# Router logits in the shared expert's unused columns, and three changes of order, in an attention and mixture-of-experts kernel on Trainium2

## The chip, the cores and the metric

The kernel runs on one core of one Trainium2 chip, as one launch. The metric is device time in microseconds. Before the change, three runs took 1483.86, 1485.7 and 1485.82 us, so the median is 1485.7 us. All times inside the kernel come from one profiled execution.

## The reference: what is computed

The input is x of 8 sequences, 512 tokens each, 256 numbers per token, all in fp32. Two residual blocks follow each other:

```python
x = x + _layernorm(attn(_layernorm(x), wq, bq, wkv, bkv, wo))
x = x + _layernorm(ffn(_layernorm(x), gate_w, w_gate, w_up, w_down, sh_gate, sh_up, sh_down))
...
# attn: 16 query heads of 128 in 4 groups, one key and value head per group, causal
q, k = q + pe, k + pe
probs = softmax(where(causal, q @ k.T / sqrt(128), -inf))
out = (probs @ v) @ wo
...
# ffn: all 4096 tokens together
scores = softmax(x @ gate_w.T)                 # 64 experts
topk_w, topk_idx = top_k(scores, 6)            # an expert takes its first 64 tokens, the rest are dropped
d = (silu(buf @ w_gate) * (buf @ w_up)) @ w_down
y = sum of the chosen experts' d, weighted
y = y + (silu(x @ sh_gate.T) * (x @ sh_up.T)) @ sh_down.T   # shared expert, 352 wide
```

## The kernel before, in words

The order of every engine's instructions is written out by hand (`manual_schedule`): the order of the Python calls is the order on PE, DVE, ACT, POOL and SP, and each engine works through its own list in order. The main loop (line 884) runs over 128 heads, k = 16 b + s with sequence b (0 to 7) and head s (0 to 15). One turn of it issues:

- `scores(k, 0..3)`, L273: the products psc (L280), DVE's e and its row minimum (L284), ACT's exponential (L287). Between the second and the third, `turned(k-1)`, L303: DVE transposes 32x32 blocks of the weights of the head before (L313), SP stores them to ex_d (L317) and loads them back as et (L320).
- `weigh(k)`, L291: reciprocal on DVE (L294), the scaling on POOL (L297).
- place A of the side work, `project(k-3)` (po, L352), place B, and a step of the routed experts where they are active (from k = 94 on).
- `queries(k+1)`, L263: the products pq (L267) and DVE's qt (L270), for which the next head's psc waits.
- `mix(k-2)`, L334: the products pav (L340) and ACT's copy ao.
- place D of the side work, and one unit of the preparation of the next sequence.

**Side work of a sequence.** `feed_forward(b-1)` makes a table of steps, keyed by head and place ("7A" is place A of head 7): residual and norm (2D to 5B), `turn` (6A: transposes pt_f into xt2, L118), `gate` (7A), `route` steps "r" (8D, 9D, 10A on) and `shared` steps "f" (8A, 8B, 9A, 9B, 11A, 11B, 12A, 13A on). `route` (L368) begins with the router's logits: 8 products pg = xt2 (stationary, 128 columns) times gw_sb (moving, 64 columns), L373, then a maximum on DVE (L376) and four exponentials on ACT (L380). `shared` (L661) computes the shared expert in chunks of 128, 128 and 96 columns (`SH_CHUNKS`): products psg and psu (L671) with the weights sg_sb and su_sb as stationary side and xt2 as moving side (512 columns), tanh on ACT (L676), two DVE products into hid (L678, L679); then the products py with sd_sb (L684). An fp32 product shows as two matmul records ("passes"), a transpose as one.

**Preparation of a sequence.** `prepare(b)` (L216) yields 12 units: load of x (`rows`), statistics (`scales`, st_a), `normal` (xn, L105), `turn` (pt_a into xnt), four `keys` (pk, L239, and kt, L242) and four `values` (pv, L250, and v, L252). For sequence 0 all 12 run ahead of the loop (L873), then `queries(0)`. For the others they run one per place: 5D, 6D, 7B (L904), 7D, 8D to 15D.

**Experts.** `experts()` (L612) works on pairs of experts from k = 94 to sequence 7's first heads; weights come by DMAs issued on ACT's queue. When all are done, `finish_early` (L864) finishes sequences 0 to 4 one after the other: SP loads two halves of y from y_d and x1 from x1_d (L650, L658), DVE adds y (L653), statistics (L76), then in `output` shift and scale on ACT (L96), POOL's additions (L641) and a store (L643).

**Tail.** `last_part` (L788) handles sequence 7 after the loop, with what is left of sequence 6 between its lines: `shared6()` is the next step of sequence 6's `shared` (8 steps, none of them done before the tail), `output6()` the next of its output, and `spare` what is left of `finish_early`. PSUM has three banks "s" (`ps_s`) and three "m" (`ps_m`); the string given to `shared` ("mmssms") says which one each of psg and psu takes.

**Loads.** SP issues x of sequence 0, then wkv, bk, bq, pe, bv, wq (one load of 2 MB), wo, gate_wt, the shared expert's weights (L146 to L159). x of a later sequence takes the buffer of the one two before it, so its load waits for that one's store to x1_d.

## Time and profile before

| | before |
|---|---|
| runs, median | 1485.7 us |
| the profiled execution's own time | 1494.1 us |
| its span, first to last instruction | 1492.3 us |
| mean granted PE clock | 0.982 |
| pg, sequences 0 to 6 (L373, 112 passes) | 13.3 us busy, 272 ns each |
| pg, sequence 7 (16 passes) | 3.9 us busy, 428 ns each |
| psg and psu (L671), mean of one pass of 512 columns | 592 ns |
| first psc, of head k = 0 | 28.29 us |
| first psc of k = 4, 16, 96, 112, 127 | 55.15, 163.33, 968.20, 1225.97, 1400.24 us |
| last po of the attention (L352) | 1418.14 us |
| last DMA issue, L643 | 1480.29 us |

Busy times are sums of the single durations, and matmuls overlap in their pipeline: 16 passes of pg start within 1.73 us though each lasts 272 ns. So the cost of products is read from start to start. In a timeline, the columns are start, duration, engine, line, operation, output and inputs, shape, count, and in brackets the idle time before and what ended it. "PEclk" is the granted share of PE's full clock; the first record of it in this execution is at 13.1 us.

### The profile page before, as it was taken

How to read it: one execution, taken by the hardware profiler on the slowest of the kernel's cores; microseconds unless marked ns; L12 is line 12 of the kernel's file. 1: busy time of each engine (PE TensorE's matmuls, PEld its weight loads, DVE VectorE, ACT ScalarE, POOL GpSimd, SP SyncE). 2: the span in 40 equal slices, each digit the busy share in tenths (PEclk: the TensorE clock that was granted, in tenths of full speed). 3: DMA queues.
4: the chain of work that ended last, by engine and by line, in shares of the span. 5: the costliest groups of instructions: out<-in, count | busy, mean ns of one | idle time of the engine just before them, and what ended most of it. 6: DMA issues, size and time to landing. Idle time of an engine off the chain costs nothing. (4 is left out here: it accounts for less than half of the span.)

```text
span 1492.3 us, 18593 instructions
## 1 busy us (share of the span) xinstructions
PE 1409.6 (94%) x5350; PEld 860.8 (58%) x5350; DVE 890.7 (60%) x3094; ACT 499.5 (33%) x1434; POOL 427.4 (29%) x682
## 2 busy tenths in 40 slices
PE   7999999999999999999999999988899998898894
PEld 3566655666656665666566666554555655565652
DVE  4565576657665676557665766665455454567442
ACT  1333343233332342233323332232333343344322
POOL 1222231124112322123112321144434344534202
PEclk9999999999999999999999999999999999999987
DMA  5764554355544464355435544469998899777511
GB/s 204 220 192 140 153 169 139 106 155 166 147 139 134 147 185 124 121 159 173 136 104 160 164 146 125 138 190 247 240 243 224 241 255 248 175 239 220 179 43 65
DMA packets 159702, 252.03 MB, mean 169 GB/s; under 512 B 16092, under 2 KB 135869, under 8 KB 159341
## 3 DMA queue, kind: packets, MB, share of 16 engines
q1 hardware_dynamic: 130061, 206.76, 46.5%
q10 hardware_dynamic: 23392, 34.61, 8.3%
q0 software_dynamic: 6144, 9.44, 3.4%
q8 instruction: 44, 0.72, 0.2%
q14 instruction: 61, 0.50, 0.1%
HBM read 143.01 MB, written 107.74 MB: 168 GB/s over the span
## 5 line engine op out<-in xcount | busy, mean ns | idle before, releaser
L297 POOL TENSOR_SCALAR e<-e,recip 128x128 f32<-128x128 f32 x508 | 269.6, 570 | 814.5 <-DVE recip L294 781.6
L287 ACT ACTIVATE e<-e,least 128x128 f32<-128x128 f32 (+3 forms) x512 | 285.8, 559 | 387.3 <-DVE least L284 356.0
L280 PE MATMUL psc<-kt,qt 128*128 128x128 f32 (+3 forms) x1024 | 312.7, 445 | 27.6 <-DVE least L284 8.7
L340 PE MATMUL pav<-et,v 128*128 128x512 f32 (+3 forms) x1024 | 297.2, 433 | 6.8 <-ACT dd L576 5.0
L340 PEld LDWEIGHTS pav<-et,v 128*128 128x128 f32 x1024 | 194.0, 190 | 170.1 <-issue 121.0
L284 DVE CUSTOM_DVE_ANT_0 e<-psc,mask 128x128 f32<-128x128 f32 (+3 forms) x512 | 231.7, 479 | 55.5 <-PE psc L280 49.6
L352 PE MATMUL po<-wo_sb,ao 128*128 128x256 f32 x1024 | 244.3, 382 | 0.7 <-ACT ao L108 0.7
L267 PE MATMUL pq<-xnt,wq_sb 128*128 128x512 f32 x512 | 240.8, 593 | 0.0
L352 PEld LDWEIGHTS po<-wo_sb,ao 128*128 128x128 f32 x1024 | 193.5, 191 | 69.3 <-issue 38.6
L280 PEld LDWEIGHTS psc<-kt,qt 128*128 128x128 f32 x1024 | 167.7, 193 | 108.7 <-DVE least L284 31.7
L313 DVE STREAM_TRANSPOSE eb<-e 128x128 f32<-128x128 f32 x756 | 227.4, 364 | 0.1
L108 ACT COPY ao<-pav 128x512 f32<-128x512 f32 x128 | 75.0, 586 | 445.3 <-PE pav L340 429.2
L270 DVE SCALAR_TENSOR_TENSOR qt<-pq,bq_sb,pe_sb 128x512 f32<-128x512 f32 x128 | 95.6, 747 | 115.0 <-PE pq L267 114.9
L267 PEld LDWEIGHTS pq<-xnt,wq_sb 128*128 128x128 f32 x512 | 95.9, 190 | 69.0 <-issue 63.5
L287 ACT ACTIVATION_READ_ACCUMULATOR e<-e,least 128x1 f32 x512 | 95.7, 187 | 0.0
L294 DVE RECIPROCAL recip<-total 128x4 f32<-128x4 f32 x128 | 22.8, 178 | 121.7 <-ACT e L287 121.7
L577 POOL DMA_INDIRECT y_d<-dd,idx x32 | 51.0, 1593 | 108.0 <-DMA y_d<-dd,idx 43.3
L239 PE MATMUL pk<-xnt,wkv_sb 128*128 128x512 f32 x128 | 61.3, 605 | 0.0
L252 DVE TENSOR_TENSOR v<-pv,bv_sb 128x512 f32<-128x512 f32 x32 | 22.1, 692 | 65.2 <-PE pv L250 65.2
L250 PE MATMUL pv<-wkv_sb,xnt 128*128 128x512 f32 x128 | 59.7, 593 | 0.0
L111 DVE COPY ht<-pth 88x256 f32<-88x256 f32 x32 | 13.4, 418 | 69.5 <-PE pth L558 69.4
L242 DVE SCALAR_TENSOR_TENSOR kt<-pk,bk_sb,pe_sb 128x512 f32<-128x512 f32 x32 | 24.0, 751 | 50.4 <-PE pk L239 50.4
(191 smaller groups left out, 1126.5 us busy)
## 6 DMA issues: line engine op xcount, KB each, us to landing
ex_d<-eb SPq DMA_DIRECT2D x126, 640.0 KB
et<-ex_d SPq DMA_DIRECT2D x504, 160.0 KB
wgu<-in_w_gate ACTq DMA_DIRECT2D x32, 352.0 KB
wgu<-in_w_up ACTq DMA_DIRECT2D x32, 352.0 KB
wd<-in_w_down ACTq DMA_DIRECT2D x32, 352.0 KB
y<-y_d SPq DMA_DIRECT2D x10, 512.0 KB
x<-in_x SPq DMA_DIRECT2D x8, 512.0 KB
x_d<-x SPq DMA_DIRECT2D x8, 512.0 KB
```

Of the source, the lines that this page charges most:

```text
L108: nc.scalar.copy(dst, src)
L239: nc.tensor.matmul(pk, lhsT=wkv_sb[:, c, g, 0, :], rhs=s["xnt"][:, c, :], start=c == 0, stop=c == NC - 1)
L250: nc.tensor.matmul(pv, lhsT=s["xnt"][:, c, ts(i, P)], rhs=wkv_sb[:, c, :, 1, :], start=c == 0, stop=c == NC - 1)
L267: nc.tensor.matmul(pq, lhsT=wq_sb[:, c, ts(h, D)], rhs=seqs[b]["xnt"][:, c, :], start=c == 0, stop=c == NC - 1)
L270: nc.vector.scalar_tensor_tensor(qt, pq, bq_sb[:, h : h + 1], pe_sb, ALU.add, ALU.add)
L280: nc.tensor.matmul(psc[:, :w], lhsT=l["qt"][:, ts(i, P)], rhs=seqs[b]["kt"][h // QPG][:, :w], start=True, stop=True)
L284: nc.vector.tensor_tensor_reduce(out=e, in0=psc[:, :w], in1=mask[:, T - w :], scale=-1.0 / math.sqrt(D), scalar=BIG, op0=ALU.add, op1=ALU. ...
L287: nc.scalar.activation(e, e, AF.Exp, bias=l["least"][:, i : i + 1], scale=-1.0, accum_out=l["total"][:, i : i + 1])
L297: engine.tensor_scalar(e, e, recip[:, n : n + 1], 1.0, ALU.mult, ALU.mult)
L313: nc.vector.transpose(blocks.rearrange("p c j t -> p j c t"), l["e"][i][:, js[0] * P : (js[-1] + 1) * P].rearrange("p (j c t) -> p j c t", ...
L340: nc.tensor.matmul(pav[:, :, j:, :], lhsT=seqs[b]["v"][:, j, ts(g, D)], rhs=l["et"][:, :, AT[j] : AT[j] + NI - j, :], start=j == 0, stop=j ...
L352: nc.tensor.matmul(po[b][i // 2][:, i % 2, :], lhsT=ao[:, ts(i, P)], rhs=wo_sb[:, h, :], start=h == 0 and i % 2 == 0, stop=h == NH - 1, sk ...
```

## The change

1. The router's weights are loaded into 32 free columns each of sg_sb and su_sb, behind the 352 of the shared expert. The chunk of 96 becomes 128 wide in psg and psu, and is now the first of the three. Its last 32 rows in each are the logits, transposed: ACT copies them into lg (64 x 512), and `route` turns them back with four transposes instead of eight products. The first chunk of `shared` moves to 7A and 7B, `gate` to 8A; this holds for sequence 6 too, whose `shared` ran in the tail entirely. In the tail, sequence 7's first chunk comes ahead of `route`.
2. Of sequence 0's preparation, only the first five units and the first values run ahead of the loop; the other six run in heads 0 to 3. wq is loaded in four parts by group.
3. 28 products of the identity with itself are put ahead of everything on PE.
4. For sequence 7 (prepared in sequence 6) the statistics move from 6D to 7D, normalization from 7B to 8B, and what follows by one place each, with one more unit at 14B. The load itself stays at 5D.
5. `spare` moves in the tail from before the last `output6()` to behind the first chunk of sequence 7.

```diff
@@ -36,6 +36,7 @@
 NEG = -3.0e38
 BIG = 3.0e38
 ROW = E + NX
+WARM = 28
 EARLY = 5
 ET_ROWS = EARLY * T
 LROW = ROW + NX
@@ -144,16 +145,24 @@
             return t
 
         x_first = load_x(0)
+
+        warm = ps_s.tile([P, T], F32, tag="s", name="warm")
+        for n in range(WARM):
+            nc.tensor.matmul(warm[:, :P], lhsT=ident, rhs=ident, start=True, stop=True)
         wkv_sb = load(wkv.rearrange("(c p) (g k d) -> p c g k d", p=P, g=G, k=2), [P, NC, G, 2, D], "wkv_sb")
         bk_sb = load(bk_t, [D, G], "bk_sb")
         bq_sb = load(bq_t, [D, NH], "bq_sb")
         pe_sb = load(pe_t, [D, T], "pe_sb")
         bv_sb = load(bv.partition_broadcast(P), [P, G * D], "bv_sb")
-        wq_sb = load(wq.rearrange("(c p) n -> p c n", p=P), [P, NC, NH * D], "wq_sb")
+        wq_sb = [load(wq[:, ts(g, QPG * D)].rearrange("(c p) n -> p c n", p=P), [P, NC, QPG * D], f"wq_sb{g}")
+                 for g in range(G)]
         wo_sb = load(wo.rearrange("(h d) e -> d h e", d=D), [D, NH, E], "wo_sb")
-        gw_sb = load(gate_wt.rearrange("(c p) n -> p c n", p=P), [P, NC, NX], "gw_sb")
-        sg_sb = load(sh_gate_t.rearrange("(c p) n -> p c n", p=P), [P, NC, FSH], "sg_sb")
-        su_sb = load(sh_up_t.rearrange("(c p) n -> p c n", p=P), [P, NC, FSH], "su_sb")
+
+        sg_sb, su_sb = [wpool.tile([P, NC, FSH + NX // 2], F32, tag=name, name=name) for name in ("sg_sb", "su_sb")]
+        for half, (t, w) in enumerate(((sg_sb, sh_gate_t), (su_sb, sh_up_t))):
+            nc.sync.dma_start(out=t[:, :, :FSH], in_=w.rearrange("(c p) n -> p c n", p=P))
+            nc.sync.dma_start(out=t[:, :, FSH:],
+                              in_=gate_wt.rearrange("(c p) n -> p c n", p=P)[:, :, ts(half, NX // 2)])
         sd_sb = wpool.tile([P, len(SH_CHUNKS), E], F32, tag="sd_sb", name="sd_sb")
         for n, (f0, fw) in enumerate(SH_CHUNKS):
             nc.sync.dma_start(out=sd_sb[:fw, n, :], in_=sh_down_t[ds(f0, fw), :])
@@ -264,7 +273,7 @@
             b, h = divmod(k, NH)
             pq = ps_m.tile([P, T], F32, tag="m", name=f"pq_{k}")
             for c in range(NC):
-                nc.tensor.matmul(pq, lhsT=wq_sb[:, c, ts(h, D)], rhs=seqs[b]["xnt"][:, c, :],
+                nc.tensor.matmul(pq, lhsT=wq_sb[h // QPG][:, c, ts(h % QPG, D)], rhs=seqs[b]["xnt"][:, c, :],
                                  start=c == 0, stop=c == NC - 1)
             qt = p2.tile([D, T], F32, tag="qt", name=f"qt_{k}")
             nc.vector.scalar_tensor_tensor(qt, pq, bq_sb[:, h : h + 1], pe_sb, ALU.add, ALU.add)
@@ -365,13 +374,12 @@
                                             imm_value=0.0)
                 yield
 
-        def route(b, xg, xt2):
-
+        def route(b, xg, l):
+
+            lg = l.pop("lg")
             pg = ps_m.tile([P, NI, NX], F32, tag="m", name=f"pg_{b}")
             for i in range(NI):
-                for c in range(NC):
-                    nc.tensor.matmul(pg[:, i, :], lhsT=xt2[:, c, ts(i, P)], rhs=gw_sb[:, c, :],
-                                     start=c == 0, stop=c == NC - 1)
+                nc.tensor.transpose(pg[:, i, :], lg[:, ts(i, P)], ident[:NX, :NX])
             most = small.tile([P, NI], F32, tag="most", name=f"most_{b}")
             nc.vector.tensor_reduce(most, pg, AX.X, ALU.max, negate=True)
             sc = p1.tile([P, NI, NX], F32, tag="sc", name=f"sc_{b}")
@@ -662,15 +670,21 @@
 
             hid = p1.tile([P, len(SH_CHUNKS), T], F32, tag="hid", name=f"hid_{b}")
             banks = iter(banks)
-            for n, (f0, fw) in enumerate(SH_CHUNKS):
+
+            for n, (f0, fw) in reversed(list(enumerate(SH_CHUNKS))):
+                mw = min(P, fw + NX // 2)
                 pgu = []
                 for w_sb, name in ((sg_sb, "psg"), (su_sb, "psu")):
                     tag = next(banks)
                     pp = {"m": ps_m, "s": ps_s}[tag].tile([P, T], F32, tag=tag, name=f"{name}_{b}_{n}")
                     for c in range(NC):
-                        nc.tensor.matmul(pp[:fw, :], lhsT=w_sb[:, c, ds(f0, fw)], rhs=xt2[:, c, :],
+                        nc.tensor.matmul(pp[:mw, :], lhsT=w_sb[:, c, ds(f0, mw)], rhs=xt2[:, c, :],
                                          start=c == 0, stop=c == NC - 1)
                     pgu.append(pp)
+                if fw < P:
+                    l["lg"] = p1.tile([NX, T], F32, tag="y", name=f"lg_{b}")
+                    on_act(l["lg"][: NX // 2, :], pgu[0][fw:, :])
+                    on_act(l["lg"][NX // 2 :, :], pgu[1][fw:, :])
 
                 gs = p2.tile([P, T], F32, tag="gs", name=f"gs_{b}_{n}", bufs=1)
                 nc.scalar.activation(gs[:fw, :], pgu[0][:fw, :], AF.Tanh, scale=0.5)
@@ -739,9 +753,12 @@
                 transpose_rows(l["xt2"], l["xg"], f"f{b}")
 
             def gate():
-                l["r"] = route(b, l["xg"], l["xt2"])
-                l["f"] = shared(b, l["xt2"], l, "mmssms" if b == B - 2 else "mmmmmm")
+                l["r"] = route(b, l["xg"], l)
                 next(l["r"])
+
+            def shared_gate():
+                l["f"] = shared(b, l["xt2"], l, "mmmmss" if b == B - 2 else "mmmmmm")
+                next(l["f"])
 
             def go(which, n=1):
                 return lambda: [next(l[which]) for _ in range(n)]
@@ -749,11 +766,11 @@
             steps = {
                 "2D": copies, "3B": lambda: scales(l["o"], "o"), "3D": residual_sums,
                 "4D": lambda: scales(xt, "f"), "5A": store, "5B": rows,
-                "6A": turn, "7A": gate,
+                "6A": turn, "7A": shared_gate, "7B": go("f"), "8A": gate,
                 "8D": go("r"), "9D": go("r"),
             }
             if b < B - 2:
-                steps |= {"8A": go("f"), "8B": go("f"), "9A": go("f"), "9B": go("f"), "11A": go("f"), "11B": go("f")}
+                steps |= {"9A": go("f"), "9B": go("f"), "11A": go("f"), "11B": go("f")}
             if b < EARLY:
                 return steps | {"10A": go("r"), "10D": go("r", 2),
                                 "11D": go("r", 2), "12A": go("f"), "12D": go("r", 2), "13A": go("f"), "13D": go("r", 2)}
@@ -805,7 +822,6 @@
                 nc.vector.bn_stats(st[:, i, :], xt[:, i, :])
             mv, rs = scales_of(st, NI, f"f{b}")
             shared6()
-            shared6()
             shift = shifts(mv, rs, f"f{b}")
             nc.sync.dma_start(out=rows_of(x1_d, b * T), in_=xt)
             xg = p1.tile([P, NI, ROW], F32, tag="xg", name=f"xg_{b}")
@@ -815,12 +831,14 @@
                 else:
                     normalize(xg[:, i, :E], xt[:, i, :], mv, rs, i)
             transpose_rows(xt2, xg, f"f{b}")
-            shared6()
-            r, f = route(b, xg, xt2), shared(b, xt2, l, "msmsms")
+            f = shared(b, xt2, l, "msmsms")
+            next(f)
+            r = route(b, xg, l)
+            for _ in spare:
+                pass
             next(r)
             shared6()
             next(r)
-            next(f)
             next(r)
             next(r)
             marked = marks(table["m"], xg[:, :, E:ROW], table["places"], b, p2, "xnt")
@@ -854,8 +872,6 @@
                 nc.vector.tensor_add(xt[:, i, :], xt[:, i, :], o[:, i, :])
                 if i % 2:
                     nc.sync.dma_start(out=rows_of(out, b * T)[:, i - 1 : i + 1, :], in_=xt[:, i - 1 : i + 1, :])
-            for _ in spare:
-                pass
             output6()
 
 
@@ -870,9 +886,14 @@
                         next(rows[b])
                 yield
 
-        for u in prepare(0):
+
+        units = list(prepare(0))
+        rest = {"0B": units[9:10], "0D": units[10:11], "1B": units[11:12], "1D": units[5:6], "2B": units[6:7],
+                "3B": units[7:8]}
+        for u in units[:5] + units[8:9]:
             u()
         queries(0)
+        assert len(units) == 12
         behind, ahead = {}, iter(())
         routed, zeroing = experts(), zeros()
         twice, finishing = False, False
@@ -880,6 +901,9 @@
 
         def side(s, place):
             behind.pop(f"{s}{place}", lambda: None)()
+            if not b:
+                for u in rest.get(f"{s}{place}", ()):
+                    u()
 
         for k in range(NK):
             b, s = divmod(k, NH)
@@ -901,7 +925,8 @@
             side(s, "B")
             if active:
                 next(routed, None)
-            if s == 7:
+
+            if s in ((8, 14) if b == EARLY + 1 else (7,)):
                 next(ahead, lambda: None)()
             if k + 1 < NK:
                 queries(k + 1)
@@ -926,7 +951,7 @@
             side(s, "D")
             if s == 5 and b + 1 < B:
                 ahead = prepare(b + 1)
-            u = next(ahead, None) if 5 <= s else None
+            u = next(ahead, None) if 5 <= s and (s != 6 or b != EARLY + 1) else None
             if u:
                 u()
             twice = active and k > EARLY * NH + NH
```

## The prediction

> **What bounds the kernel now.** I read the page first (busy shares, the 40 slices), then the waits of PE, then the timelines at the places that the diff touches.
>
> ```profile
> PE 1409.6 (94%) x5350; PEld 860.8 (58%) x5350; DVE 890.7 (60%) x3094; ACT 499.5 (33%) x1434; POOL 427.4 (29%) x682
> ...
> PE   7999999999999999999999999988899998898894
> PEclk9999999999999999999999999999999999999987
> DMA  5764554355544464355435544469998899777511
> ```
> Each digit is a tenth of a slice of 37 us. PE and its clock: PE is the bound for the first two thirds, so each pass taken off it there is worth its length. From some 1000 us on DMA is at 8 to 9 tenths, and PE has holes. The holes by cause:
>
> ```profile
> PE psc L280 <- DVE least L284: 8.7, 7, 1.3
> PE pt_a L118 <- DVE xn L105: 8.3, 1, 8.3
> PE psc L280 <- DVE qt L270: 8.2, 11, 3.2
> PE pd L567 <- DMA wd<-in_w_down: 6.5, 2, 4.4
> ...
> PE psc L280 <- DVE ht L111: 6.0, 2, 4.4
> ```
> The columns are total, times, longest. The 8.3 is the start, where PE has nothing to do until the first rows are loaded and normalized; the 4.4 under ht is one event, at 1056.8 us.
>
> **Start: products, split queries, keys and values between heads.** PE's timeline of before:
>
> ```profile
> 8.29 2.30 PE L118 MATMUL pt_a<-ident,xn 128*128 128x128 f32 x8 [8.29 <-DVE xn L105]
> 10.41 8.45 PE L239 MATMUL pk<-xnt,wkv_sb 128*128 128x512 f32 x16
> 18.70 7.03 PE L250 MATMUL pv<-wkv_sb,xnt 128*128 128x512 f32 x16
> ```
> Four keys units are 16 passes: an fp32 product is two. Weight loads of pk come 0.86 us apart until 13.12 and 0.43 after: the first passes ran at half clock, though the clock column says 1.00 (no record yet). A unit is 4 passes, 1.72 us. The first keys end at 13.55; then 7 units (12.0), pq (1.72) and qt (0.95) make the first psc at 28.3, as seen (28.29).
>
> The 28 products are 56 passes of 128 columns, 0.108 us at full clock and 0.215 at half (psc's 2,560 columns take 2.32 and, at 1389 us, 4.63). ident is ready at 1.82. [...] By the row alone (2.7 us from 10.41 to 13.1) they would end near 9. PE is in order, so pt_a queues behind them, and ACT and DVE wait for pt_a. I take 10.3: transposes 0.86, copies 0.8, first keys done at 13.4 against 13.55. So the products themselves gain about 0 (+0.9 to -1.2).
>
> Then pv (1.72), pq (1.72), qt (0.95): first psc at 17.8. wq's first quarter must be there at 15: with x, wkv and the small loads it is 2.6 MB, and 253 GB/s in the first 10 us bring it by 10.5. SP issues four more loads (4 x 0.45 us, done near 20); its next duty is ex_d, near 28.
>
> The six units (10.3 us) go into heads 0 to 3, in which PE idled 0.84, 1.81, 1.79 (+0.8 behind pq at 27.4), waiting for qt. By PE's sums heads 0 and 1 become 7.4 (from 4.99, 5.95), head 2 becomes 7.8 (8.16), head 3 9.5 (7.76): 32.0 instead of 26.9 to head 4's psc. DVE's extra 0.7 per unit (v, kt) is within 0.4 us of PE's pace. Head 4 at 49.8 instead of 55.15: **-5.3** (-3 to -7).
>
> **Gate in the shared expert's columns.** Each of sequences 1 to 7 has, at s=7,
>
> ```profile
> 223.77 1.89 PE L373 MATMUL pg<-gw_sb,xt 128*128 128x64 f32 x16
> 225.50 1.95 PE L352 MATMUL po<-wo_sb,ao 128*128 128x256 f32 x8
> ```
> 16 passes in 1.73 us (223.77 to 225.50), 0.108 each: 64 columns cost what 128 do. psg and psu of the 96-wide chunk become 128 wide: the moving side stays 512 columns, so nothing on PE. Added: four transposes of 64 rows, one pass each; not in the trace. Bounds 0.2 (half the rows) and 0.9 (half clock); nearest row pt_a, 8 in 0.87, so 0.43. Saved 1.3 a sequence.
>
> Added on ACT: two copies of 512 columns (0.59 each), ahead of tanh. Behind them: tanh, DVE's two hid products, then normal (2.2), then qt, for which PE waits. From the head at 221.5: exps done 226.8, psu ends 227.1, copies 228.0, tanh 228.6, hid 230.1, xn 232.2, qt 232.9; PE, with psg and psu moved in (+3.43) and pg out, needs qt at 233.6. So the copies cost nothing, with 0.7 us of cover (what it costs without it is the rival below). Head 8 loses 3.43 and gains 0.43. pg, most and exps move a head later, next to 8D: ACT is done at S+7.5, before pav's copy at S+8. Five sequences: **-6.5**; the sixth lies where DMA is near its limit: **-0.9** (0 to -1.3).
>
> **The last rows.** DVE and PE, sequence 6, heads 6 and 7:
>
> ```profile
> 1058.97 1.41 DVE L76 BATCH_NORM_STATS2 st_a<-x 128x6 f32<-128x256 f32 x4 [5.97 <-DMA x<-in_x]
> ```
> ```profile
> 1061.24 3.75 PE L280 MATMUL psc<-kt,qt 128*128 128x256 f32 x6 [4.44 <-DVE ht L111]
> ```
> SP issues x at 1050.03, behind the store of x_d (1041.29); DVE stands at st_a until 1058.97, and with it ht, gxt and e of the next head; PE loses 4.44 and then 3.4 us at half clock (1.7). The load stays where it is and st_a moves from 6D to 7D, some 18 us on: the wait is gone. Turn, keys and values follow one slot later and end at 15D as before. What is late next is DMA: the experts' weights had this hole to catch up in. Bounds 0 and -6.1; slices without a hole ran at DMA shares of 0.8 to 1.1, PE at 100%, so some slack exists: **-4.5**.
>
> **Sequence 7, head 7.** Here the moved chunk comes out of the tail into a head whose DVE also adds y (finish). Before: recip 1321.4, y, statistics, qt to 1326.3. After: tanh at 1323.35, hid to 1324.75, y and statistics (3.2) to 1328.0, qt 1328.7: **+2.4**. Head 8's extra 0.43 is met by head 9's wait for y<-y_d (1.56 on DVE, 3.3 on PE), which shrinks by it: 0.
>
> **Tail.** With one chunk gone (3.43), PE runs out at 1427 instead of 1430.4 before pt_f at 1432, which DVE's chain (statistics, x, st_f) sets and which stays. PE's clock there:
>
> ```profile
> 1428.00:1432.00 4.00, 2.46 (x7) 0.68 (x5) 3.79 (x15) 0.39 (x1) 1.01 (x1) 1.00 0.36 131
> 1432.00:1436.00 4.00, 3.24 (x13) 2.39 (x14) 1.60 (x4) 1.77 (x4) 0.00 (x0) 0.63 0.00 0
> 1436.00:1440.00 4.00, 4.00 (x17) 3.73 (x17) 1.03 (x2) 0.90 (x7) 0.00 (x0) 0.50 0.01 2
> 1440.00:1444.00 4.00, 4.00 (x12) 3.20 (x12) 3.03 (x19) 0.39 (x4) 0.00 (x0) 0.59 0.21 79
> ```
> (PE busy is the second figure, the granted clock third from the end.) [...] The row shows that 1.5 us of idleness already halved it: I take 0. The chunk that now follows is 512 columns wide, 6 of its 8 passes slow: 34.0 to 40.0 (1400 left out), copies 40.8, transposes 41.3, y's products (32 passes, 6.9) 48.2, the places' products 48.8 instead of 51.8. ACT's part (tanh, the four scales of the spare 2.1, exps 1.3) ends near 45, DVE's choice at 48.2: just in time. The chunk's PSUM bank is held until after the places, so the second half of y waits for pg's bank, free at 45 when PE wants it at 44.8: 0, and 1 to 2 if the scales delay the exps more. So -3.0, and the same work behind it. At the end:
>
> ```profile
> 1475.83 1.29 SPq L856 DMA_DIRECT2D out_dram<-x  x2
> 1480.29 0.92 SPq L643 DMA_DIRECT2D out_dram<-x  x2
> ```
> The two L643 stores stand behind the spare (shift, scales, POOL's adds 1477.5 to 1480.3), now done earlier; one of them remains, right after L856: 3.3 more on SP, of which the store's own landing leaves 2.5. Together **-5.5** (-2 to -7).
>
> **Sum.** 5.3 + 6.5 + 0.9 + 4.5 - 2.4 + 5.5 = 20.3. The profiled execution took 1494.1 (span 1492.3, 1.8 around it): 1473.8. The runs' median is 1485.7, 8.4 below it; I carry the difference over: **1465.4**.
>
> **Rivals.**
> - DMA takes the hole back: sequence 6 gives nothing (5.4 less), 1471. For it: the slices; against: 100 us without a wait for wd after the hole. 0.17.
> - The start gives nothing, the products ending after 13: 1471. For it: the half clock; against: even all-slow they end at 13.9. 0.08. With the former 1476: 0.06.
> - The waits for y<-y_d in sequence 7 dissolve, since its heads shift: 3.3 idle and 1.7 of half clock at one or two of them: 1456 to 1460. 0.09.
> - Slower: tanh at s=7, now behind two copies, holds hid, xn and qt on DVE in six heads. It has 0.7 us of cover; every idleness over some 2 us costs 1.7 of half clock too. It decides from 2.9 us of delay on: 2.2 idle, 6 x (2.2 + 1.7) = 23 against the 20 gained; 4.1 gives 6 x (3.4 + 1.7) = 31: 1496. Near 2.5 it is no change. For it: DVE waits there already (0.30 for gs at 237.9); against: the count above. 0.07, and 0.04 for no change.
> - That the change doesn't do what it says: the half clock stays in the tail and the transposes queue behind y: 3 to 5 less, 1469. In the range.
>
> **How the numbers follow.** The forecast as worked out has 0.49, its own range 1460 to 1471. To leave out no more than 2 in 10, the range takes in the first four cases: 1456 to 1477. A measurement here tells 0.2% (3 us). Faster 0.89, within 0.2% 0.04, slower 0.07.
>
> **What would show it.** Heads: psc of head 4 near 50; s=7 of sequences 1 to 5 longer by 1.7 and s=8 shorter by 3.0; no wait for x<-in_x at sequence 6; x2 stores of L643 gone from the end. Wrong if psc waits for qt at head 8's start, if pd waits for wd appear past 1080, or if pt_a ends after 12.

## The result and the profile after

| | runs | median, us | lowest to highest | ratio to before, 95% interval | profiled execution (span) |
|---|---|---|---|---|---|
| before | 20 | 1489.77 | 1483.86 to 1494.24 | 1 | 1494.1 (1492.3) |
| after | 20 | 1477.67 | 1472.42 to 1483.77 | 0.9925 [0.991, 0.994] | 1482.25 (1480.5) |

The change takes 12.1 us off, where 20.3 were forecast: the right sign, and 12.3 us above the forecast's 1465.4. Of these, 4.1 are the yardstick, since over 20 runs the kernel before has a median of 1489.8 and not 1485.7; 8.2 are gain that did not come. The two profiled executions are among the slower ones of their kernels (before 4.3 above the median, after 4.6), so what follows by stage compares one execution with one. The page of after, for busy shares and slices:

```profile
PE 1404.6 (95%) x5310; PEld 853.3 (58%) x5310; DVE 887.2 (60%) x3094; ACT 507.5 (34%) x1450; POOL 424.8 (29%) x682
...
PE   9999999999999999999999999989899999899985
...
DMA  7664554355444554445435554459999889668711
```

PE is busy 5.0 us less. Its digits are full from the first slice on, and PE still has holes where DMA stands at 8 to 9 tenths. The waits of PE in after (total, times, longest):

```profile
PE psc L289 <- DVE least L293: 12.1, 10, 2.5
PE psc L289 <- DVE qt L279: 6.4, 4, 3.4
PE pd L575 <- DMA wd<-in_w_down: 5.8, 3, 2.7
...
PE pgu L549 <- DVE gs L692: 3.7, 1, 3.7
```

The 8.3 of the start is gone. "least" (DVE, late with a head's row minimum) has grown from 8.7 to 12.1, and its longest from 1.3 to 2.5. A wait of pgu for gs has appeared. Both stand in the stages where the gain is missing.

**Start.** PE's timeline of after:

```profile
1.87 8.33 PE L151 MATMUL warm<-ident 128*128 128x128 f32 x56 [1.87 <-POOL ident masks.py:199]
10.04 1.04 PE L119 MATMUL pt_a<-ident,xn 128*128 128x128 f32 x8
...
17.57 2.42 PE L289 MATMUL psc<-kt,qt 128*128 128x128 f32 x8 [0.84 <-DVE qt L279]
```

The clock rose at 5.7 us (its first record is at 5.71; the passes start 0.21 us apart before and 0.11 after), so 17 passes were slow. The products end near 10.2. The forecast's 10.3 was the author's estimate; the profile of before does not show it, and the row that the forecast reads gives near 9. The first psc is at 17.57 (17.8), heads 0 to 3 take 7.41, 7.31, 7.77 and 9.48 (7.4, 7.4, 7.8, 9.5), and head 4 starts at 49.54 (49.8).

**Gate.** In head 24 the four transposes have taken the place of the 16 passes:

```profile
232.35 0.46 PE L382 MATMUL pg<-ident,lg 64*128 64x64 f32 x4
232.74 1.99 PE L361 MATMUL po<-wo_sb,ao 128*128 128x256 f32 x8
```

They cost 0.39 us from start to start (forecast 0.43). The wider chunk costs PE nothing, as forecast: in before a pass took 592 ns with 96 columns of weights as with 128, and in after psu starts 1.71 us behind psg in the widened chunk (219.80, 221.51) as in a chunk of 128 before (234.58, 236.29).

**By stage**, from the starts of the heads. The last three columns are experiments 7 and 8, told below: the same two kernels, each with one store issued sooner.

| heads | forecast | before | after | difference | before, sooner store | after, sooner store | difference |
|---|---|---|---|---|---|---|---|
| up to head 4 | -5.3 | 55.15 | 49.54 | -5.6 | 54.80 | 49.83 | -5.0 |
| 4 to 15 | 0 | 108.18 | 109.68 | +1.5 | 108.41 | 108.96 | +0.6 |
| 16 to 95 (sequences 1 to 5) | -6.5 | 804.87 | 804.68 | -0.2 | 804.67 | 798.65 | -6.0 |
| 96 to 111 (sequence 6) | -5.4 | 257.77 | 255.71 | -2.1 | 249.93 | 250.03 | +0.1 |
| 112 to 126 (sequence 7) | +2.4 | 174.27 | 174.79 | +0.5 | 174.68 | 173.29 | -1.4 |
| 127 to the end | -5.5 | 92.06 | 86.10 | -6.0 | 90.51 | 84.54 | -6.0 |
| span | -20.3 | 1492.3 | 1480.5 | -11.8 | 1483.0 | 1465.3 | -17.7 |

Start and tail came near their forecasts. Two rows failed: in these executions sequences 1 to 5 gave nothing, and sequence 6 gave less than half.

**Where the gate's gain went.** The worst place is head 55, 16.56 us long where the like heads take 12.3. DVE, then PE:

```profile
539.08 1.40 DVE L77 BATCH_NORM_STATS2 st_a<-x 128x6 f32<-128x256 f32 x4 [3.06 <-DMA x<-in_x]
```
```profile
541.22 1.74 PE L289 MATMUL psc<-kt,qt 128*128 128x512 f32 x2 [2.53 <-DVE least L293]
```

It is the wait for x at 6D, the one that the forecast knew from sequence 6 alone, now in sequence 3 (for the x of sequence 4). DVE stands at st_a; the row minima of the next head are queued behind it; PE runs dry for 2.53 us; then the granted clock halves. The windows of after around it (PE busy is the second figure, the granted clock the third from the end):

```profile
538.00:541.60 3.60, 1.07 (x4) 0.37 (x3) 2.49 (x14) 0.40 (x3) 0.55 (x1) 1.00 0.54 219
541.60:545.00 3.40, 3.40 (x5) 1.35 (x4) 2.70 (x10) 1.86 (x7) 0.46 (x1) 0.50 0.98 246
```

Why x is late there: its load is issued when the store of the x two before (L743, to x1_d) has landed. SP's queue in after:

```profile
527.71 0.38 SPq L743 DMA_DIRECT2D x_d<-x  x1
534.66 0.40 SPq L144 DMA_DIRECT2D x<-in_x  x1
```

The load is 6.95 us behind the store, where the other four sequences take 4.2 to 4.6. The traffic of DMA from 527 to 535 us, in 40 slices of 0.2 us:

```profile
DMA  3998989789879999999752200000000000000000
GB/s 109 301 320 320 326 192 211 179 192 166 152 198 286 259 300 334 367 399 435 266 174 72 78 6 6 13 13 23 26 26 20 26 26 26 5 0 0 0 0 0
```

From 531.6 on the share rounds to 0, and until 533.9 the rest of the store trickles out at 6 to 26 GB/s, one packet after another (from 532.56 on 1,024 bytes every 42 to 43 ns): about a sixteenth of the 320 to 435 that all 16 engines moved together until 531, 20 to 27 each by that estimate. At 530.64, in the middle of the store, the trace has a packet of 16,384 bytes of the queue that the page calls "instruction". The experiments take this up.

This execution is the worst of its kind. In the eight other profiles that have the gate in its new place and the store and the statistics of these sequences in their old ones, heads 16 to 95 take 800.6 to 803.4 us: there the gate brings 1.5 to 4.3 against the 804.87 of before, and not the 6.0 that it brings when DVE does not wait (the last columns).

### The profile page after: what moved, and what is told of

Its sections match the earlier page's. It is cut to its first block, busy times and chain, and to the rows that moved or that the text cites. A ratio compares the mean times of both kernels' runs of the same rounds, so it can differ in the third digit from the quotient of the medians.

```text
span 1480.5 us, 18545 instructions
## 1 busy us (share of the span) xinstructions
PE 1404.6 (95%) x5310; PEld 853.3 (58%) x5310; DVE 887.2 (60%) x3094; ACT 507.5 (34%) x1450; POOL 424.8 (29%) x682
## 5 line engine op out<-in xcount | busy, mean ns | idle before, releaser
L306 POOL TENSOR_SCALAR e<-e,recip 128x128 f32<-128x128 f32 x508 | 266.2, 557 | 802.6 <-DVE recip L303 775.1
L289 PE MATMUL psc<-kt,qt 128*128 128x128 f32 (+3 forms) x1024 | 311.2, 441 | 24.3 <-DVE least L293 12.1
```

The source lines that it names most:

```text
L289: nc.tensor.matmul(psc[:, :w], lhsT=l["qt"][:, ts(i, P)], rhs=seqs[b]["kt"][h // QPG][:, :w], start=True, stop=True)
L306: engine.tensor_scalar(e, e, recip[:, n : n + 1], 1.0, ALU.mult, ALU.mult)
```

## Experiments

The edits are against the kernel after, unless said otherwise.

**1. The slot of the statistics undone.**

```diff
-if s in ((8, 14) if b == EARLY + 1 else (7,)):
+if s == 7:
-u = next(ahead, None) if 5 <= s and (s != 6 or b != EARLY + 1) else None
+u = next(ahead, None) if 5 <= s else None
```

> The changed kernel with the fourth edit undone: sequence 7's statistics are back at 6D, the rest as changed. Theory (DMA takes the hole back): in the changed kernel's trace head 103 still idles 3.97 us, now because ACT stands behind its weight loads and pgu behind a PSUM bank, so the later slot is worth little: this is at most 2 us slower than the changed kernel, ratio to before 0.992 to 0.994. Rival (the slot is worth what the prediction gave it, and the loss lies elsewhere): 4 to 6 us slower, ratio 0.995 to 0.997.

1478.22 us (22 runs), ratio 0.9937 [0.9922, 0.9951]; after has 0.9925 [0.991, 0.994]. DVE's wait for x is back (6.53 us), and heads 96 to 111 take 253.6 all the same, no longer than after's 255.7. DVE in this kernel:

```profile
1047.52 1.41 DVE L77 BATCH_NORM_STATS2 st_a<-x 128x6 f32<-128x256 f32 x4 [6.53 <-DMA x<-in_x]
```

So taking that wait away was not worth 4.5 us here.

**2. The later slot in every sequence.** It takes the waits for x away everywhere.

```diff
-if s in ((8, 14) if b == EARLY + 1 else (7,)):
+if s in (8, 14):
-u = next(ahead, None) if 5 <= s and (s != 6 or b != EARLY + 1) else None
+u = next(ahead, None) if 5 <= s and s != 6 else None
```

> The changed kernel with the statistics of every next sequence at 7D instead of 6D, not only of the last. Theory (DVE's wait for x at 6D costs in the first six sequences: 1.6, 0.5, 0.6, 3.1, 0.5, 1.0 us in the changed kernel's trace against 0, 0.3, 0.2, 0.2, 0.2, 0.4 before): no wait for x is left in any sequence, heads 7 of sequences 0 and 3 lose their 0.92 and 2.53 us of idle PE; 3 to 6 us faster than the changed kernel, ratio 0.988 to 0.990. Rival (those waits are chance of one execution and DVE's later work takes their place at 7D): within 1 us of the changed kernel, ratio 0.992 to 0.993.

1477.43 us, 0.9944 [0.9923, 0.9965]. No wait for x is left, and nothing is gained: in each sequence heads 7 and 8 take 20.41, some 2.4 less than in after, and heads 9 to 15, into which keys and values are pushed back, take 2.75 more. Moving the waiting instruction has a price of its own; the expected gain did not come.

**3. The logits' copies behind tanh**, so that hid does not wait for them (sequence 7 left as it is).

```diff
-if fw < P:
+def logits():
     l["lg"] = p1.tile([NX, T], F32, tag="y", name=f"lg_{b}")
     on_act(l["lg"][: NX // 2, :], pgu[0][fw:, :])
     on_act(l["lg"][NX // 2 :, :], pgu[1][fw:, :])
 
+if fw < P and b == B - 1:
+    logits()
 gs = p2.tile([P, T], F32, tag="gs", name=f"gs_{b}_{n}", bufs=1)
 nc.scalar.activation(gs[:fw, :], pgu[0][:fw, :], AF.Tanh, scale=0.5)
+if fw < P and b < B - 1:
+    logits()
```

> The changed kernel with the two copies of the logits behind tanh on ACT instead of ahead of it (sequence 7 excepted). Theory (the copies hold tanh, and with it DVE's hid and the PSUM banks, in sequence 6, where pgu waits 3.7 us for gs): that wait falls to about 2.5, in the first sequences nothing changes, since qt has cover there: 1 to 2 us faster than the changed kernel, ratio 0.991 to 0.992. Rival (the copies are hidden everywhere): no difference, 0.9925. Rival (they cost in every sequence): 5 us or more, below 0.989.

1478.39 us, 0.9943 [0.9922, 0.9963]: no difference that can be told. The wait of pgu for gs fell further than expected, and nothing was gained:

```profile
PE pgu L549 <- DMA wgu<-in_w_up: 2.6, 1, 2.6
...
PE pgu L549 <- DVE gs L696: 1.1, 1, 1.1
```

A wait for a load of weights stands in its stead. The place of ACT's copies is not what costs the missing gain.

**4. No products of the identity.**

```diff
-warm = ps_s.tile([P, T], F32, tag="s", name="warm")
-for n in range(WARM):
-    nc.tensor.matmul(warm[:, :P], lhsT=ident, rhs=ident, start=True, stop=True)
```

> The changed kernel without the 28 products. Theory (PE works through them until 10.2 us, 1.0 after xn is complete, and gains the half clock back): first psc at 17.0 to 18.5 against 17.57, the time within 1 us of the changed kernel, ratio 0.992 to 0.993. Rival (they are what the start's gain comes from): 3 us slower, 0.9945.

1480.11 us, 0.9943 [0.9927, 0.9959]; first psc at 17.78 against 17.57. That is no difference: in the other profiles with 28 products it lies between 17.3 and 18.7. The products are worth about nothing at the start, as the forecast had it. But they did something else: without them head 55 is normal, and it is the x loaded in head 70, sequence 4, that is late (5.33 us from store to load). The same packets fall elsewhere, roughly 17 us later against the work. That led to the next two.

**5. and 6. The number of products, to move the packets.**

```diff
-WARM = 28
+WARM = 20
```

> The kernel after with 20 products of the identity ahead of all instead of 28; nothing else changes. It is a test of what made one x late in sequence 4's side work (x issued 6.95 us behind the store to x1_d that it waits for, in head 54, where the others take 4.0 to 4.6). Theory: 16 KB packets of the queue for instructions come every 256 instructions or so of PE; one of them at 2.9 us into that store stretched it. With 16 passes less (32 records with their weight loads, at 0.15 us each by the kernel without products) every such packet comes 4.9 us later relative to the work: 7.8 us behind the store of head 53 (clear: the distance falls back to 4.0 to 4.6, heads 55 and 56 from 27.0 to about 24) and 2.5 us behind the store of head 21 (hit: its distance grows from 4.2 to 5.3 to 7, heads 23 and 24 longer by 1 to 3). Rival: the long distance is chance, or comes from the load of x, wo or other traffic at that place: head 54 stays late, head 22 stays at 4.2. The time is within 0.2% of after by both.

> The kernel after with 12 products of the identity instead of 28. By the theory of the instruction packets they come 9.8 us later relative to the work and hit none of the stores: 8.9, 7.4, -9.8, 12.7, -5.4 and 14.3 us from the stores of sequences 0 to 5. Then all distances from store to load of x are 4.0 to 4.6, heads 16 to 95 take about 802 (after 804.7), and the time is 2 to 3 us below after. Rival (chance): one of the distances is 5.5 or more again, or heads 16 to 95 stay at 804.7. The start: first psc at 17.6 to 18.2 as with 28.

Times 1475.28 and 1475.41 us, ratios 0.9898 [0.9875, 0.992] and 0.9895 [0.9873, 0.9918]. From the store's issue to the packet, and to the load of x (us; only packets within 6 us are given):

| sequence of the store | after (28) | 20 products | 12 products |
|---|---|---|---|
| 1 | -2.4, load at 4.17 | **+1.99, load at 5.76** | +4.60, load at 4.54 |
| 2 | none, 4.62 | none, 4.50 | none, 4.25 |
| 3 | **+2.93, load at 6.95** | +4.80, load at 4.83 | +5.13, load at 4.66 |
| 4 | none, 4.38 | none, 4.55 | -5.66, load at 4.33 |
| 5 | +4.48, load at 4.24 | +4.63, load at 4.30 | none, 4.21 |

(Sequence 3's store is the one in head 54; the expectation counted by the x that is loaded, sequence 4's.) With 20 products the long store moved from sequence 3 to sequence 1, as the theory said and the rival (chance, or other traffic at head 54) did not; with 12 none is long, and heads 16 to 95 take 800.6 (expected 802). The packets moved less evenly than expected (4.80 where 7.8 was worked out), and with both numbers of products smaller waits of DVE for x stay (up to 1.2 us). In the kernel with 20 products, SP's queue and DVE:

```profile
205.34 0.38 SPq L743 DMA_DIRECT2D x_d<-x  x1
211.10 0.40 SPq L144 DMA_DIRECT2D x<-in_x  x1
```
```profile
215.63 1.41 DVE L77 BATCH_NORM_STATS2 st_a<-x 128x6 f32<-128x256 f32 x4 [2.00 <-DMA x<-in_x]
```

The store was issued at 205.34 and the load at 211.10; x landed 4.5 us later and found DVE 2.00 us idle.

**7. The store of x issued sooner** (at 4B instead of 5A: 7.5 us ahead of the start of head 6 instead of 0.1 behind it); neither the load nor the statistics move.

```diff
-"4D": lambda: scales(xt, "f"), "5A": store, "5B": rows,
+"4B": store, "4D": lambda: scales(xt, "f"), "5B": rows,
```

> The kernel after with the store of x to x1_d issued at place 4B instead of 5A, about 12 us sooner; the load of x stays at 5D. It takes away what the load waits for, without moving the statistics or the keys. Theory: what the gate's move did not bring in heads 16 to 95 is DVE's wait for x at 6D (0.5 to 0.6 us in four sequences, 3.06 in one, 1.6 in the first): without it these heads take 801 to 802 instead of 804.7, and the pairs of heads 7 and 8 (43.3, 41.4 and so on with the gate) are each 1.0 shorter than before, none longer. Time 2.5 to 3.5 below after. Rival: the transposes or the logits' copies cost the rest: no change in heads 16 to 95.

1467.19 us, **0.9854 [0.983, 0.9878]**: faster than after, and beyond the expectation of 2.5 to 3.5 us. SP's queue at the same place as above, and DVE:

```profile
519.14 0.38 SPq L743 DMA_DIRECT2D x_d<-x  x1
...
527.82 1.70 SPq L144 DMA_DIRECT2D x<-in_x  x1
```
```profile
534.94 1.40 DVE L77 BATCH_NORM_STATS2 st_a<-x 128x6 f32<-128x256 f32 x4
```

There are 8.7 us between store and load, so even a long store is through; the load is issued when its own place comes, some 3.5 us sooner in the head than where it waits for the store, and st_a carries no bracket: DVE does not wait. Heads 16 to 95 take 798.65, below the 801 to 802 expected.

**8. The same sooner store in the kernel before.**

> The kernel before with the store of x to x1_d at place 4B instead of 5A; nothing of the change is in it. It asks whether the sooner store helps any kernel by as much, or mainly the one whose heads the change has tightened. Theory: before, DVE waits only 0.2 to 0.35 us for x in sequences 1 to 5, which PE's pair of heads 7 and 8 hardly shows: heads 16 to 95 fall from 804.9 to 803.5 to 804.5; the 5.3 us wait of sequence 6 shrinks to about 1, which is worth up to 4. Together 1 to 5 below before (ratio 0.9966 to 0.9993); so the change, between the two kernels with the sooner store, is worth 17 to 21 us, near the forecast's 20.3. Rival: it is worth as much here as in the changed kernel (8 us, ratio 0.9945): the change alone is then worth the 12 that were measured, and the gate's term was wrong in itself.

1484.22 us, 0.9956 [0.9941, 0.9971]. That is 6.0 us, a little over the 1 to 5 of the theory and under the rival's 8. By stage nearly all of it lies in sequence 6 (249.9 against 257.8 and, in the second profile of before, 253.3); heads 16 to 95 are unchanged (804.67). Between the two kernels with the sooner store the change is worth 17.0 us by medians, 15.2 by the ratios and 17.7 by profiles: at or under the low end of what was expected (17 to 21).

Over all profiles of these kernels one rule gives heads 7 and 8 of a sequence together, from DVE's wait for x at 6D (w, us): 23.73 with the old gate and 22.53 with the new one, plus w - 0.26 where that is above zero. Some of the rows (measured, rule):

| kernel, sequence | w | heads 7 and 8 | by the rule |
|---|---|---|---|
| before, 1 | 0.32 | 23.79 | 23.79 |
| before again, 5 | 1.09 | 24.56 | 24.56 |
| before with the new start, 3 | 1.59 | 25.06 | 25.06 |
| before, sooner store, 1 to 5 | 0 | 23.72 to 23.73 | 23.73 |
| after, 1 | 0.49 | 22.75 | 22.76 |
| after, 5 | 0.98 | 23.25 | 23.25 |
| after, 3 (windows above) | 3.06 | 27.02 | 25.33 |
| 20 products, 1 | 2.00 | 24.27 | 24.27 |
| after, sooner store, 1 to 5 | 0 | 22.52 to 22.53 | 22.53 |

Of 75 such pairs in 15 profiles (2. has its statistics elsewhere) only two leave the rule by more than 0.01 us. One is after's 27.02: 1.69 more, the half clock that follows the hole. The other, 0.27 more, is a pair of experiment 3, where the copies stand elsewhere.

**9. Sooner store and statistics back at 6D** (7. and 1. together).

> The kernel after with the sooner store (4B), and the statistics of sequence 7 back at 6D. If the slot of the statistics has no worth of its own and DMA or x's landing sets heads 96 to 111: within 0.2% of the kernel with the sooner store alone (1467.2), heads 96 to 111 at 249 to 252. If the slot is what takes the wait away, a wait for x of 3 to 6 us comes back at head 102, heads 96 to 111 take 253 to 256 and the time is 3 to 5 us above 1467.2.

1471.86 us, 0.9887 [0.9865, 0.9908], against 0.9854 [0.983, 0.9878] with the later slot: 4.7 us above by medians, in another series of runs, and the intervals just overlap. The wait for x in sequence 6 is 0.72 us here, so whatever the slot is worth beside the sooner store does not come from that wait. In the two profiles the difference lies in heads 112 to 118 (96.5 against 91.0), behind the slot and not in it. The one other kernel with the sooner store and these statistics at 6D (8.) takes 95.5 there, and all others with the full load of weights 89.7 to 93.7. Neither of the expectations fits; why is open.

**10. The start alone, in the kernel before.** The edit is that part of the change's diff.

> The kernel before with the start's part of the change alone (28 products of the identity, wq in four loads, six units of sequence 0 between heads 0 to 3). The forecast's term and its measured size agree: head 4's first psc at 49.5, 5.6 below before, and the time 5.3 to 5.6 below before (ratio 0.9963), if the parts add up. Rival: DMA or instruction packets give part of it back later: 3 or less.

1487.93 us, 0.9992 [0.9978, 1.0007]: the rival's side. Head 4 starts at 50.1, 5.1 sooner than before; heads 4 to 15 give 0.7 back and heads 16 to 95 3.3 (808.2), all of it in waits for x: 1.59 us in sequences 1 and 3, where a packet comes 2.4 us ahead of the store and the store itself is issued 0.7 late. In this profile the kernel gives back 4.0 of the start's 5.1 by head 95, at places that nobody touched; over all its runs no gain can be told. (The profiled execution, 1480.65, is the fastest: heads 96 on, which the edit leaves as they were, happened to be short in it.)

**11. The gate alone, in the kernel before**: item 1 of the change with the tail's order of chunks, without the start, the later statistics and the spare's new place.

> The kernel before with the gate in the shared expert's columns alone (item 1 with the tail's new order of chunks; not the start, the slot of the statistics, nor the place of the spare finish). The forecast's terms give -6.5 - 0.9 - 3.0 + 2.4 = -8.0. By the readings so far each of sequences 1 to 5 gives 1.2 where DVE doesn't wait for x, and about 0.4 less for 0.5 us of that wait: heads 16 to 95 at 801 to 803 (-2 to -4), heads 119 and 120 +2.9, tail -2 to -3: 2 to 5 us below before (ratio 0.9966 to 0.9987). Rival: the gate alone gives the 8 (ratio 0.9946).

1488.41 us, 0.9988 [0.9972, 1.0004], the weak end of the expectation. Heads 16 to 95: 803.4; DVE waits 0.6 to 1.8 us for x in all five sequences, and by the rule that leaves 1.5 of the 6.0. The two longest waits have a packet at the store: 1.77 us behind its issue in sequence 4, 2.4 ahead of it in sequence 2. Heads 119 and 120 +2.9; tail 88.7, 3.4 below the first profile of before and 2.3 below the second.

**12. The kernel before once more**, for a second profile.

> The kernel before once more, for a second profile. Its first profile is one of the longer of its runs (1494.1 against a median of 1489.8). Open: how much of what looked like a gain in heads 101 to 102 (36.7) and in the tail (92.1 from head 127 on) was that execution's own. If chance: heads 101 to 102 at 31 to 35 and the tail at 88 to 91 here. If not: within 0.5 us of the first.

1485.21 us. Heads 101 and 102 take 31.6 (first profile 36.7), heads 121 to 126 60.5 (66.0), the tail 91.0 (92.1). So 5 us in each of the first two were that execution's own: a comparison of one profile with one profile would have called them gains or losses of the change. The tail varies too: experiment 10, whose tail is that of before, takes 87.7 there (the reason stands below, under the tail).

**13. and 14. Lighter DMA, with both slots.** These two kernels leave out one of the two loads of each early pair of experts (w_up) and use the gate's weights in its place, so their routed experts' result is not the reference's. The work of the engines stays. By the pages DMA moves 240.5 MB instead of 252.0: 11.5 MB less (the expectation's 22 is too high). 14. has the edit of 1. besides.

```diff
-for k, w in enumerate((w_gate, w_up)):
+for k, w in enumerate((w_gate, w_up) if key == "late" else (w_gate,)):
 ...
+both = l["wgu"][:, e, :, c, :]
+if key != "late":
+    both = l["wgu"][:, e, 0:1, c, :].to_broadcast([P, 2, F])
 ...
-rhs=l["wgu"][:, e, :, c, :]
+rhs=both
```

> The kernel after without the load of the routed experts' up-weights (one of the two loads of each pair; the products use the gate's weights for both, so that PE's, ACT's and DVE's work stays; the late pairs keep their loads): some 22 of the 66 MB of the experts' weights left out, and with it the routed experts' result. Statistics of sequence 7 at 7D. If DMA sets heads 96 to 118: the waits for wd, for gx and ex_d and of ACT behind its own loads shrink, heads 96 to 118 take 330 to 338 (347.8 in after), and the time is 10 to 17 us below after (1461 to 1468). If PE and DVE set them anyway: within 3 us of after.

> The same without the up-weights, with the statistics of sequence 7 back at 6D. It asks where the 4.5 us went that the forecast gave the slot. If DMA takes the hole back when it is loaded (the rival of the forecast), the slot is worth its price once DMA has room: x still lands behind its wait at 6D (3 to 5 us of DVE's wait), so this one is 3 to 5 us slower than the same kernel with 7D. If x lands in time here, since DMA is light, the wait is gone in both and both take the same. If neither: the slot has no worth of its own, whatever DMA does, and the forecast had the wrong idea of what follows the wait.

1453.88 us (0.9756 [0.9723, 0.9789]) and 1456.54 (0.977 [0.9737, 0.9804]). Heads 96 to 118 take 322.7 and 324.6 instead of 347.8: 25 and 23 us, more than expected. The window from 1040 to 1060 us, heads 102 and 103 in both, of after, and then of 13.:

```profile
1040.00:1060.00 20.00, 15.98 (x68) 8.74 (x68) 8.42 (x28) 6.93 (x17) 9.97 (x13) 0.93 0.98 246
```
```profile
1040.00:1060.00 20.00, 19.90 (x94) 11.25 (x91) 11.47 (x43) 8.84 (x22) 8.56 (x10) 1.00 1.00 241
```

The same DMA share, and PE 15.98 of 20 us in the one and 19.90 in the other: with less to load for each pair, PE is the bound again. In both light kernels x lands in time: with 6D st_a follows 0.73 us behind the experts' hid, and the profile puts that down to hid, not to x. Heads 96 to 111 take 242.46 with 7D and 242.47 with 6D. So in its own heads the slot has no worth beyond the wait (the second of the three cases expected; in the profiles the difference of the two lies in heads 112 to 126, and the intervals overlap). With all the weights the wait was there, and undoing the slot in the kernel after still cost nothing (1.): DMA sets these heads, and a hole that is taken away reappears elsewhere, as in 3.

## Why the prediction was wrong, step by step

Two steps failed: "the copies cost nothing, with 0.7 us of cover", under the five sequences' -6.5, and "so some slack exists", under the -4.5 of the later statistics.

**"Five sequences: -6.5"**. What the gate itself saves was nearly right: without waits for x the gate gives 23.73 - 22.53 = 1.20 us a sequence (forecast 1.3), 6.0 in all, as the right half of the table shows; head 7 is 1.65 longer and head 8 is 2.85 shorter (forecast 1.7 and 3.0). So the copies cost 0.1 at most. What failed is the cover: the count began at head 7 with x taken as landed. The waits of DVE for x, before and after (total, times, longest):

```profile
DVE st_a L76 <- DMA x<-in_x: 9.6, 7, 6.0
```
```profile
DVE st_a L77 <- DMA x<-in_x: 9.5, 7, 3.1
```

The forecast used the 6.0 and left the other six unread. In before they are 2.3 for the very first rows, and 0.2 to 0.35 in each of sequences 1 to 5, such as this one:

```profile
220.66 1.41 DVE L76 BATCH_NORM_STATS2 st_a<-x 128x6 f32<-128x256 f32 x4 [0.32 <-DMA x<-in_x]
```

That is at the edge of the 0.26 that PE does not feel. So there was no cover left at this place before the change, and any lateness of x goes to PE one for one. In after the waits are 0.49 to 3.06: by the rule 4.3 us, plus 1.7 of half clock, which is the whole of the gate's 6.0 (and 1.3 more in sequence 0, most of the 1.5 that heads 4 to 15 lost). Why x became later is settled for the largest part of this execution's loss, the long store under a 16 KB packet (4.5 of the 6.0; 5. and 6.). The smaller waits, up to 1.7 us where no packet fell 1.3 to 2.9 us behind the store, stay open in part; the second profile of before has them too (0.28 to 1.09).

The packets of the instruction queue, on the page of after (0.72 MB in 44 packets, so 16 KB each):

```profile
q8 instruction: 44, 0.72, 0.2%
```

From one packet to the next PE works through 255 instructions (passes, weight loads and waits; 254.6 to 255.9 on average in each of the 16 profiles), and taking PE instructions away moved the packets. A packet can cost something: beside one that took 1.0 us, the store took 6.95 instead of 4.2. How it delays the store was not seen, nor why 1.0 us of packet makes 2.7 of delay.

**"So some slack exists: -4.5"** (and the -0.9 of sequence 5's gate). Wrong; the rival "DMA takes the hole back", given 0.17, had this term right. The slices with DMA at 0.8 to 1.1 and PE at 100% were read as slack, when they were stretches in which PE happened to have its data; without w_up's loads these heads lose 25 us (13.). In after the wait for x at sequence 6 is gone and PE stands somewhere else:

```profile
1051.93 0.40 ACT L296 ACTIVATE e<-e,least 128x128 f32<-128x128 f32 x1 [5.58 <-DMA wd<-in_w_down]
```
```profile
1059.18 2.62 PE L549 MATMUL pgu<-wgu,gxt 128*64 128x352 f32 x8 [3.74 <-DVE gs L692]
```

ACT stands until 1051.93 behind its own loads of weights, its exponentials, lg's copies and tanh come late, DVE's gs with them, and PE waits 3.74 us for the bank that gs frees. Over the profiles with the new gate and full DMA, heads 96 to 126 take 427.7 to 431.8 with the statistics at 6D and 423.3 to 433.4 at 7D.

**"Head 4 at 49.8: -5.3"**. Right: -5.6, and each time inside it within 0.3 us; the products' "gain about 0" too (4.). Not foreseen was that this part moves the packets against the stores (10.).

**"Sequence 7, head 7: +2.4"**. Right in kind: head 119 takes 2.3 more. Head 120's 0.6 more was not met by the wait for y, as had been forecast; heads 121 to 126 take 4.0 less, but 5.5 of the 66.0 that they took was that execution's own (12.).

**Tail "-5.5"**. Near, with some luck: -6.0 in both pairs, of which 1.7 is the clock's. From the end of the last po to the places' products it took 27.9 us (forecast 28.8, before 31.2), and of these 6.8 were at half clock, where before had 10.2. After's windows there:

```profile
1424.00:1428.00 4.00, 1.78 (x8) 1.40 (x8) 2.26 (x8) 1.65 (x3) 1.01 (x1) 0.71 0.39 137
1428.00:1432.00 4.00, 4.00 (x7) 1.85 (x6) 0.76 (x2) 0.13 (x2) 0.00 (x0) 0.50 0.00 0
1432.00:1436.00 4.00, 3.33 (x13) 1.59 (x12) 0.42 (x1) 2.47 (x5) 0.20 (x1) 0.94 0.00 0
```

In before the clock stayed at half until 1443. But that is chance: the four profiles with the old order of the tail have the same hole of 1.54 us ahead of pt_f, with 10.2, 6.8, 6.8 and 0 us of half clock behind it, and the stretch took 26.8 to 31.2 us. The windows of the last of these, experiment 10:

```profile
1420.00:1424.00 4.00, 2.02 (x7) 0.57 (x5) 2.99 (x12) 1.47 (x3) 1.01 (x1) 1.00 0.38 131
1424.00:1428.00 4.00, 3.60 (x25) 3.06 (x25) 2.39 (x4) 0.71 (x3) 0.00 (x0) 1.00 0.00 0
```

So the prediction's reading, that 1.5 us of idleness halves the clock, held in three executions of four. With the change the stretch takes 26.3 to 27.9. What is steady is the part behind it, 41.1 before and 38.5 after, the forecast's 2.5. There one L651 store is left behind the last pair:

```profile
1467.95 1.29 SPq L874 DMA_DIRECT2D out_dram<-x  x2
1469.33 0.46 SPq L651 DMA_DIRECT2D out_dram<-x  x1
```

**The sum.** By the spans 11.8 of the 20.3 came. Missing are 6.3 in heads 16 to 95, 3.3 in sequence 6 and 1.5 in heads 4 to 15; start, sequence 7 and tail gave 2.7 more than forecast, the tail's and sequence 7's share within what two executions of one kernel differ by. The prediction's slower rival, tanh behind two copies, was wrong in its cause (3.) but not in its place: DVE in head 7 was the chain without cover. Its "every idleness over some 2 us costs 1.7 of half clock too" is answered in the last section: half clock followed in 68 of 69 steps with 2.05 us or more of idle PE, but not behind every such hole.

**The best version** is the change with the sooner store: 1467.19 us, 0.9854 of before, one line changed. It is 10.5 us below after by medians. In the profiles it takes 6.0 less in heads 16 to 95 (2.0 to 4.7 against the other profiles with the gate in its new place) and 5.7 less in heads 96 to 111. The first part is explained; for the second there is one profile each, in a stretch that varies by 9 us between two executions of before (432.0 and 422.9 for heads 96 to 126). That stays open.

## What to carry to other kernels

Before counting a saving as worth its length, look in the same heads for an engine that already waits for a transfer, however shortly: a wait at the edge of its cover takes the saving one for one. The remedy is to issue what the load waits for sooner, not to move the work that waits: in the kernel after, the sooner store brought 10 us, the later statistics nothing that could be told. And where DMA sets the pace, a hole on PE is not a gain waiting to be taken; ask first whether it goes away when the transfers are made lighter.

## What was not expected of the hardware

- A packet of 16,384 bytes of the instruction queue comes about every 34 us, and it can lengthen a 512 KB store. The 13 profiles with the store at 5A have 65 such stores in sequences 1 to 5. Nine had a packet 1.3 to 2.9 us behind the store's issue, and the load that waits for it followed 5.3 to 7.0 us behind the store; the other 56 took 4.2 to 4.8. In ten, with a packet some 2.4 us ahead, the store itself was issued 0.3 to 0.7 us later than is usual. The packets follow PE's instruction count (255 from one to the next), so an edit at the start of a program changes a wait 500 us later.
- The clock does not go by the length of a hole alone. In each of the 16 profiles the clock records change on a grid of 3.41 us. Counted over all of them from PE's records, a step of 3.41 us at full clock with 2.05 us or more of idle PE in it was followed by half clock in 68 of 69 cases, one with 1.75 to 2.05 in 16 of 31, and one with less in 1 of 6,588 (experiment 12's tail, with 1.36). So the 2.53 us in head 55, all in one step, cost 1.7 us, a hole of 2.16 us at the same place in 14. cost nothing beyond itself, and the tail's 1.54 us, with small gaps beside it, lie at the edge.
- One profile is not enough for the stretch that DMA sets: two executions of the same kernel differ there by 9 us, while PE's own stretches (58.2 and 78.9 us) repeat to 0.02.
